# A graph network on one core: the attention's first rows and masks are kept in places of the row work and loaded during the second convolution

## The chip, the cores and the metric

The kernel runs on one core of a Trainium2 chip. The metric is the device time of one execution in microseconds (us), as the median of several runs. The engines are named as in the profile: PE is TensorE (PEld its weight loads), DVE is VectorE, ACT is ScalarE, POOL is GpSimd, and SP is SyncE, which here only issues DMAs. A "q" behind a name (SPq) is the engine's instruction queue.

## The reference

There are N = 6250 nodes with D = 128 features and E = 100000 edges, sorted by their end `dst`. Two graph convolutions run one after the other, then an attention layer; both parts add their input and normalise each row.

```python
def gcn_conv(x, src, dst, ew, W, b):          # with a self loop of weight 1 per node
    deg = segment_sum(ew, dst, N)
    dinv = where(deg > 0, rsqrt(deg), 0)
    h = x @ W
    return segment_sum(h[src] * (dinv[src] * ew * dinv[dst])[:, None], dst, N) + b

h  = sigmoid(gcn_conv(relu(gcn_conv(x, ..., W1, b1)), ..., W2, b2))
x1 = layernorm(x + h)
z, rh = x1 @ fc_w.T, edge_attr @ fc_r_w.T     # attention; aw is attn_w in three rows
e = leaky_relu(z[src] @ aw[0] + z[dst] @ aw[1] + rh @ aw[2], 0.01)
alpha = softmax of e over the edges with the same dst
out = relu(segment_sum(alpha[:, None] * (z[src] + rh), dst, N) + x1 @ loop_w)
return layernorm(x1 + out)
```

## The kernel before

The edges are cut into NC = 49 chunks of CC = 2048, the nodes into NB = 49 blocks of 128 (P). For each chunk, `pick` gathers the source rows in two ways: most of them from a table in SBUF (`hot`, three bfloat16 parts per value) by matmuls with a 0/1 matrix (`mask`, L532, product `g`), the rest by indirect DMA issued by POOL (`far`, L541). `pick` also builds `wm` (L547, L554), the 0/1 matrix of the edges' ends. `scatter` (L578) multiplies the gathered rows with it into a window of 144 nodes, and `add_in` (L583) adds this window to the accumulator. `weigh` (L571) puts the edge weights in. Chunk c is picked while chunk c-1 is scattered. This is done three times: in the first convolution, in the second and in the attention ("conv3").

Whenever a window has moved past some nodes, a `Pieces` object deals out the work that these nodes need next, as generators. `x1_of` is that of the second convolution, for up to four blocks of nodes at a time: multiply by `dinv` (L329), sigmoid (L440), transpose (L444), add (L446), normalise (L411 to L418), transpose (L454), the products with the attention's weights (L463), copies (L466, L467), the product with the loop weights (L471), and the three parts of the next `hot` table (ACT L476, DVE `low` L479 to L481, store `hz` L482). The last two pieces can only be done when the last chunk has been added in.

The second convolution also carries two kinds of work for the attention: `edge_dots` (L1030, L1031), which multiplies each edge's attributes with a vector, and `row_work`, a generator with one step for each of the first chunks. It loads `dst` and `src` by rows, and writes `drow` and `srow` to DRAM (node number within its block, for the ends and the sources), and `rels`, `place` and `blks` to SBUF. Its large tiles are `h_i`, `d_i`, `s_i`, `s_j` (in turn in one place, tag "i", 8 KB in each partition), `h_f`, `d_f` (tag "f", 8 KB) and `s_b` (4 KB), all from the pool `rows2`, which is closed with the second convolution.

The attention's scores are a generator too, `scores`, which runs ahead of the chunks. `ends(c0, n)` loads `dk`, four chunks of `drow` broadcast to all partitions (L1110), compares it with the partition number (L1112), multiplies with the table `a_d` (L1117) and stores `adg` to `adgd`. `starts(c)` does for each half chunk: `sources` loads `rk`, 1024 values of `srow` broadcast (L1105, two half chunks ahead), a comparison (L1138), `ohb` (L1140), 24 matmuls `k` with `adp` (L1145), a product and a sum (`sel`, L1148). `softmax(b)` takes a batch of chunks (2, 5, then 7) from there to `al3` and `aw`, the attention of its edges in two layouts. `shares` (L1254 to L1264) and `edge_part` (L1275 to L1304) use them chunk by chunk, and `pick`, `scatter` and `add_in` work as before with `mask` loaded from `masks` (L1325).

The pools give each tile its number of buffers: three `rk`, one `dk`, two `al3`, two `mask`, two `ohb`.

At the start, the tiles `spread` and `spread_f` (about 1 KB together in each partition) hold a permutation of the partitions, from which `first` (L169) is made. Then the pool `prep` loads `dst_i` (SP), `ew_f` (ACT), `src_i` (SP) and the weights (ACT, L610), and casts `dst_f` (L616, L617), from which `ends` (L622) and all the sorting follow.

What sets the order: outside the second convolution's loop a scheduler orders the instructions of each engine, from its own estimates; only the start of the scores has raised priority. The loop of the second convolution is in `manual_schedule`, in the order in which it is written. Every engine executes its instructions in order, and a wait holds up all that stand behind it.

Of the kernel before, what the change touches and what calls it, by code (L numbers as in the profile page):

```python
# [9 lines left out]
F32 = mybir.dt.float32  # L10
# [9 lines left out]
P = 128  # L20
# [5 lines left out]
TC = 16  # L26
# [12 lines left out]
def gnn_kernel(ctx, tc, x, src, dst, ea, ew, W1, b1, W2, b2, fcw, fcrw, attn, loopw, out):  # L39
# [119 lines left out]
    nc.gpsimd.tensor_copy(behind[:, : P - 1], ident[:, 1:])  # L159


    spread = const.tile([P, P + 1], I32, name="spread")
    for of, at in ((iota_i[:, :P], slice(0, P)), (iotap_i[:, 0:1], slice(P, P + 1))):
        nc.vector.tensor_scalar(spread[:, at], of, 79, None, op0=OP.mult)
        nc.vector.tensor_scalar(spread[:, at], spread[:, at], P - 1, None, op0=OP.bitwise_and)
    spread_f = const.tile([P, P + 1], F32, name="spread_f")
    nc.vector.tensor_copy(spread_f, spread)
    first = const.tile([P, P], BF16, name="first")
    nc.vector.tensor_scalar(first, spread_f[:, :P], spread_f[:, P:], None, op0=OP.is_gt)  # L169

    lower = const.tile([P, TC, TC], BF16, name="lower")
    nc.vector.tensor_tensor(lower, iotab[:, None, :TC].to_broadcast([P, TC, TC]),
# [768 lines left out]


    acc2 = acc1
    with tc.tile_pool(name="conv2", bufs=2) as wp, tc.tile_pool(name="arp", bufs=2) as ap_, \
            tc.tile_pool(name="rows2", bufs=1) as rp, tc.tile_pool(name="x1p", bufs=2) as xp, \
            tc.tile_pool(name="ps_g2", bufs=4, space=PSUM) as ps_g, \
# [1 line left out]


        def row_work():  # L950
            h_i = rp.tile([P, NT, P + 2], I32, name="h_i", tag="i")
            nc.gpsimd.memset(h_i, -1)
            for b, (c0, n) in enumerate(batches):

                at = lambda r: (c0 * NL + r - 1) * P - 1
                rows = [r for r in range(n * NL + 2) if at(r) >= 0 and at(r) + P + 2 <= E]
                r0, m = rows[0], len(rows)
                nc.sync.dma_start(h_i[r0 : r0 + m, b, :], bass.AP(tensor=dst.tensor, offset=dst.offset + at(r0), ap=[[P, m], [1, P + 2]]))
                if b == 0:
                    nc.sync.dma_start(h_i[1:2, b, 1:], dst[None, 0 : P + 1])  # L960
                if b == NT - 1:
                    for r in range(r0 + m, n * NL + 2):
                        if at(r) < E:
                            nc.sync.dma_start(h_i[r : r + 1, b, : E - at(r)], dst[None, at(r) : E])
            yield
            h_f = rp.tile([P, NT, P + 2], F32, name="h_f", tag="f")
            nc.vector.tensor_copy(h_f, h_i)

            nc.vector.scalar_tensor_tensor(same, h_f[:, :, 1:], -0.5, h_f[:, :, : P + 1], op0=OP.max, op1=OP.is_equal)
            yield  # L970
            nc.vector.tensor_scalar(last, same[:, :, 1:], -1.0, 1.0, op0=OP.mult, op1=OP.add)

            filled = rp.tile([P, NT], F32, name="filled")
            nc.vector.tensor_reduce(filled, same[:, :, 1:P], AX.X, OP.min)
            nc.vector.tensor_reduce(odd[:, 3:4], filled, AX.X, OP.max)
            yield
            d_i = rp.tile([NC, CC], I32, name="d_i", tag="i")
            load_rows(nc.sync, d_i, dst)
            yield
            d_f = rp.tile([NC, CC], F32, name="d_f", tag="f")  # L980
# [12 lines left out]
            yield  # L993
            nc.vector.tensor_tensor(dp, dp, off[:, :, None].to_broadcast([NC, NL // 2, 2 * P]), op=OP.subtract)
            offc = rp.tile([NC, NL // 2], F32, name="offc")
            nc.vector.tensor_tensor(offc, off, off[:, 0:1].to_broadcast([NC, NL // 2]), op=OP.subtract)
            yield
            nc.vector.tensor_reduce(odd[:NC, 2:3], d_f, AX.X, OP.max)
            nc.vector.tensor_scalar(odd[:NC, 2:3], odd[:NC, 2:3], float(WS), None, op0=OP.is_ge)
            yield  # L1000
            by_partition(ps_mm, lambda t, ps: nc.scalar.copy(rels[:, :, t], ps), lambda t: ds_[:, t, :])
            ps = ps_mm.tile([P, NL // 8, 64], F32, name="mm")
            for s in range(NL // 2):
                q = s % 4
# [4 lines left out]
            s_i = rp.tile([NC, CC], I32, name="s_i", tag="i")  # L1009
            load_rows(nc.sync, s_i, src)  # L1010
            yield
            nc.vector.tensor_scalar(s_i, s_i, 127, None, op0=OP.bitwise_and)
            s_b = rp.tile([NC, CC], BF16, name="s_b")
            nc.vector.tensor_copy(s_b, s_i)
            nc.sync.dma_start(srow[:, :], s_b)
            yield
            s_j = rp.tile([NC, CC], I32, name="s_j", tag="i")
# [62 lines left out]
    with tc.tile_pool(name="look", bufs=2) as lp, tc.tile_pool(name="conv3", bufs=2) as wp, \  # L1080
# [2 lines left out]
            tc.tile_pool(name="ps_r3", bufs=1, space=PSUM) as ps_r, tc.tile_pool(name="ps_k3", bufs=1, space=PSUM) as ps_k, \  # L1083
            tc.tile_pool(name="ps_c3", bufs=2, space=PSUM) as ps_c:
        MB = max(n for _, n in batches)
        zero = lp.tile([1, P], F32, name="zero", bufs=1)
        nc.vector.memset(zero, 0.0)
        nc.sync.dma_start(adgd[None, 0:P], zero)
        nc.sync.dma_start(adgd[None, (NC * NL + 1) * P :], zero)

        a_d = lp.tile([P, 3, J, NB], BF16, name="a_d", bufs=1)
        for j in range(J):
            ps = ps_c.tile([P, 3, NB], F32, name="rec")
            nc.tensor.matmul(ps, wide[:, P + j : 2 * P + j], adp[:, 1, :, :NB], start=True, stop=j == 0)
# [6 lines left out]
        def sources(i):  # L1101

            if i < 2 * NC:
                rks[i] = lp.tile([P, HC], BF16, name="rk", bufs=3)
                nc.sync.dma_start(rks[i], srow[i // 2, None, i % 2 * HC : (i % 2 + 1) * HC].to_broadcast([P, HC]))  # L1105

        def ends(c0, n):

            dk = lp.tile([P, 4 * P], BF16, name="dk", bufs=1)
            nc.sync.dma_start(dk[:, : n * P], drow[c0 : c0 + n, :].rearrange("(o c) p -> o (c p)", o=1).to_broadcast([P, n * P]))  # L1110
            yield
            nc.vector.tensor_scalar(dk[:, : n * P], dk[:, : n * P], iotap, None, op0=OP.is_equal)  # L1112
# [19 lines left out]
        def starts(c):  # L1132

            for h in range(2):
                of = slice(h * NL // 2, (h + 1) * NL // 2)
                sources(2 * c + h + 2)
                mk = rks.pop(2 * c + h)
                nc.vector.tensor_scalar(mk, mk, iotap, None, op0=OP.is_equal)  # L1138
                ohb = lp.tile([P, NB, NL // 2], BF16, name="ohb")
                nc.vector.tensor_tensor(ohb, iota_t[:, :NB, : NL // 2], blks[:, c, None, of].to_broadcast([P, NB, NL // 2]),  # L1140
                                        op=OP.is_equal)
                ps = ps_k.tile([P, NL // 2, NB], F32, name="k")
                for s in range(NL // 2):
                    for k in range(3):
                        nc.tensor.matmul(ps[:, s, :], mk[:, s * P : (s + 1) * P], adp[:, 0, k, :NB], start=k == 0, stop=k == 2)  # L1145
                yield
                sel = lp.tile([P, NL // 2, NB], F32, name="sel", bufs=1)
                nc.vector.tensor_mul(sel, ps, ohb.rearrange("p b s -> p s b"))  # L1148
                nc.vector.tensor_reduce(asr[:, 1 + c * NL + of.start : 1 + c * NL + of.stop], sel, AX.X, OP.add)
# [3 lines left out]
        def softmax(b):  # L1153
# [65 lines left out]
            yield  # L1219
            aw = lp.tile([P, MB * NL], F32, name="aw")  # L1220
            nc.scalar.copy(aw[:, : n * NL], ps[:, 1 : R - 1])
            al3 = lp.tile([P, MB, TC, 3], BF16, name="al3")
            parts(lambda k: al3[:, :n, :, k], al[:, :n, :], nc.vector)
            ready[b] = al3, aw.rearrange("p (c s) -> p c s", s=NL)

# [83 lines left out]
        for b, (c0, n) in enumerate(batches):  # L1309
# [6 lines left out]
            for c in range(c0, c0 + n):  # L1316
# [4 lines left out]
                    deal(to - done)  # L1321
                    done = to

                mask = wp.tile([P, GP * P], BF16, name="mask", bufs=2)
                nc.sync.dma_start(mask, masks[c])  # L1325
                shares(c, al3, c - c0)
                beside()
# [15 lines left out]
        pieces.go(N, 999)  # L1343
    right_r.close()
    rightA.close()
    hotp.close()


# [174 lines left out]
```

## Time and profile before

| | |
|---|---|
| runs, us | 2397.48, 2405.32, 2406.43, 2407.49, 2418.14 (median 2406.43) |
| profiled execution | 2418.03 us, of which the span is 2416.1 us |
| mean granted TensorE clock | 0.836 |
| busy in the span | PE 1837.7 us, DVE 1659.5, POOL 1043.9, ACT 957.2 |
| DMA | 316.38 MB, mean 131 GB/s |
| stages of the span | start and sorting to 176 us, first convolution to 866, between to 912, second convolution to 1447, between to 1482, scores of the first batch to 1550, attention to 2410 |

How to read it: busy times are sums over one execution, by engine. A stage's own row tells more than the whole: between the stages no engine is busy, and the time is that of a chain in which one waits for the other. The chain of waits follows the work back from the last instruction; a line "DMA a<-b" in it is a transfer that somebody waited for. In the timeline, "[2.75 <-X]" is the idle time of that engine before the instruction and what ended it.

### The profile page before, as it was taken

The page shows a single profiled execution, that of the slowest core. Times are in us where ns is not written, and L with a number is a line of the kernel's source. Part 1 is how long each engine was busy: PE and PEld are TensorE (multiplying, and loading weights), DVE is VectorE, ACT ScalarE, POOL GpSimd, SP SyncE. Part 2 cuts the span into 40 slices and gives each one's busy share as a digit, 9 for nine tenths or more (in the row PEclk, how much of TensorE's full clock was granted, in tenths as well). Part 3 has the DMA queues.
Part 4 walks back from the last instruction along what each step waited for, and adds up shares of the span by engine and source line. Part 5 has one row for each costly group of instructions (what it writes and reads, how often), then busy time and mean ns, then how long its engine had stood idle before and what let it go on. Part 6 is the DMA issues. An engine that isn't in the chain of part 4 may idle for free.

```text
span 2416.1 us, 79261 instructions
## 1 busy us (share of the span) xinstructions
PE 1837.7 (76%) x34061; PEld 1604.9 (66%) x34061; DVE 1659.5 (69%) x3281; ACT 957.2 (40%) x3099; POOL 1043.9 (43%) x941
## 2 busy tenths in 40 slices
PE   3767888878888758788878884587877778888884
PEld 2556777767777647677667673577766767767774
DVE  7895776766767337777777775887876777776552
ACT  1253444443443425465556552033323232424332
POOL 4054345544444526576666652123332233324441
PEclk9778788878888868898888895678888888889887
DMA  2132314232231456666566575446444455544441
GB/s 54 29 109 80 107 52 137 56 119 90 79 121 51 135 182 197 181 187 205 181 191 204 178 204 158 123 115 157 134 145 129 141 139 150 143 133 130 129 131 47
DMA packets 257393, 316.38 MB, mean 131 GB/s; under 512 B 38349, under 2 KB 194131, under 8 KB 249466
## 3 DMA queue, kind: packets, MB, share of 16 engines
q1 hardware_dynamic: 224823, 249.62, 32.8%
q0 software_dynamic: 23520, 48.22, 9.4%
q10 hardware_dynamic: 8688, 13.37, 1.7%
q8 instruction: 270, 4.42, 0.8%
q14 instruction: 92, 0.75, 0.1%
HBM read 265.14 MB, written 45.97 MB: 129 GB/s over the span
## 4 chain that ended last, share of the span: by engine, by line
PE 62%; DVE 14%; issue 13%; ACT 4%; another core or an unknown queue 4%; DMA 2%; POOL 0%; DVEq 0%; ACTq 0%; SPq 0%; POOLq 0%
PE win L578 24%; PE g L532 19%; PE r L758 3%; PE rec L1263 2%; PE r L1293 2%; DVE sel L1148 2%; PE rec L821 2%; PE k L1145 2%; PE rec L1304 2%; ACT got L537 2%; DVE wm L547 1%; DVE put L814 1%; PE mm L383 1%; DVE ohm L809 1%
## 5 line engine op out<-in xcount | busy, mean ns | idle before, releaser
L541 POOL DMA_INDIRECT far<-g,sidx x490 | 694.0, 1416 | 574.5 <-PE win L578 415.0
L532 PE MATMUL g<-hot,mask 128*32 128x128 bf16 x21168 | 578.9, 250 | 279.0 <-issue 257.8
L537 ACT ACTIVATE got<-g,swt 128x128 f32<-128x128 f32 x1764 | 493.5, 377 | 654.8 <-PE g L532 223.2
L532 PEld LDWEIGHTS <-mask 128*32 128x32 bf16 x21168 | 426.8, 111 | 398.2 <-issue 381.0
L541 POOL DMA_INDIRECT far<-zd,sidx x245 | 295.2, 1205 | 631.6 <-PE win L578 526.6
L578 PE MATMUL win<-wm,got 128*128 128x144 f32 x3528 | 556.1, 317 | 10.1 <-DVE acc L583 6.3
L578 PEld LDWEIGHTS win<-wm,got 128*128 128x128 f32 x3528 | 517.6, 215 | 35.3 <-issue 20.5
L547 DVE TENSOR_TENSOR wm<-iota,sdst 128x1728 f32<-128x1728 f32 x147 | 286.6, 1950 | 1.1 <-POOL hot L343 0.8
L571 ACT ACTIVATE wm<-wm,swt 128x64 f32<-128x64 f32 (+1 forms) x735 | 200.8, 353 | 75.3 <-DVE wm L554 38.8
L583 DVE TENSOR_TENSOR acc<-acc,win 128x144 f32 x147 | 44.6, 303 | 218.9 <-PE win L578 211.3
L578 PE MATMUL win<-wm,far 128*128 128x64 f32 (+1 forms) x1470 | 184.4, 272 | 0.0
L578 PEld LDWEIGHTS win<-wm,far 128*128 128x128 f32 x1470 | 180.6, 194 | 0.2 <-ACT got L537 0.2
L1145 PE MATMUL k<-adp,rk 128*128 128x49 bf16 x2352 | 105.6, 200 | 63.9 <-DVE sel L1148 34.7
L1145 PEld LDWEIGHTS <-rk 128*128 128x128 bf16 x2352 | 93.0, 107 | 81.7 <-issue 54.4
L1030 DVE TENSOR_TENSOR et<-et,ar_row 128x2048 f32<-128x2048 f32 (+1 forms) x49 | 111.6, 2278 | 5.4 <-DMA et<-in_edge_attr_dram 5.4
L1031 DVE TENSOR_REDUCE dots<-et 128x16 f32<-128x2048 f32 (+1 forms) x49 | 112.0, 2286 | 1.7
L1148 DVE TENSOR_TENSOR sel<-k,ohb 128x392 f32<-128x392 f32 x98 | 83.8, 855 | 23.2 <-PE k L1145 12.1
L758 PE MATMUL r<-oh,first 128*128 128x48 bf16 x784 | 79.7, 268 | 9.0 <-DVE oh L754 8.0
L809 DVE TENSOR_TENSOR ohm<-iota_t,pm 128x2048 bf16<-128x2048 bf16 x49 | 59.7, 1219 | 38.2 <-PE rec L821 33.3
L1298 ACT COPY sw<-r 128x256 f32<-128x256 f32 (+1 forms) x49 | 18.3, 374 | 161.2 <-PE r L1293 81.5
L758 PEld LDWEIGHTS <-first 128*128 128x128 bf16 x784 | 69.5, 120 | 15.9 <-issue 6.3
L814 DVE TENSOR_TENSOR put<-ohg,rec 128x1360 bf16<-128x1360 bf16 x49 | 77.8, 1588 | 0.0
(408 smaller groups left out, 2295.8 us busy)
## 6 DMA issues: line engine op xcount, KB each, us to landing
et<-in_edge_attr_dram SPq DMA_DIRECT2D x97, 512.0 KB
et<-in_edge_attr_dram SPq DMA_DIRECT2D x48, 1024.0 KB
mask<-masks SPq DMA_DIRECT2D x98, 384.0 KB
rk<-srow SPq DMA_DIRECT2D x98, 256.0 KB
mask<-srd SPq DMA_DIRECT2D x49, 384.0 KB
masks<-mask SPq DMA_DIRECT2D x49, 384.0 KB
far<-g,sidx POOLq DMA_INDIRECT x490
dr<-dinvd SPq DMA_DIRECT2D x22, 256.0 KB
```

The source lines that it names most:

```text
L532: nc.tensor.matmul(ps[32 * q : 32 * q + 32, g, :], mask[:, (g0 + g) * P + 32 * q : (g0 + g) * P + 32 * q + 32], hot[:, 4 * (g0 + g) + q, k ...
L537: nc.scalar.activation(got[:, g, :], ps[:, g, :], AF.Copy, scale=swt[:, c, g0 + g : g0 + g + 1])
L541: nc.gpsimd.indirect_dma_start(out=got, out_offset=None, in_=table[:, :], in_offset=bass.IndirectOffsetOnAxis(ap=sidx[:, c, g : g + 1], ax ...
L547: nc.vector.tensor_tensor(wm[:, : GP * WC].rearrange("p (g w) -> p g w", w=WC), iota[:, None, 1 : WC + 1].to_broadcast([P, GP, WC]), sdst[ ...
L571: nc.scalar.activation(m, m, AF.Copy, scale=swt[:, c, g : g + 1])
L578: nc.tensor.matmul(ps[:, n0 : n0 + m.shape[-1]], rows[g], m, start=g == 0, stop=g == G - 1)
L758: nc.tensor.matmul(ps, first, oh[:, :, t], start=t == 0, stop=t == TC - 1)
L814: nc.vector.tensor_tensor(put[:, :, : G * F].rearrange("p t (g f) -> p t g f", f=F), ohg[:, :, :, None].to_broadcast([P, TC, G, F]), rec[: ...
L1030: nc.vector.tensor_mul(et[:n], et[:n], ar_row[:n, None, :].to_broadcast([n, TC, D]))
L1031: nc.vector.tensor_reduce(dots[:n, c, :], et[:n], AX.X, OP.add)
L1145: nc.tensor.matmul(ps[:, s, :], mk[:, s * P : (s + 1) * P], adp[:, 0, k, :NB], start=k == 0, stop=k == 2)
L1148: nc.vector.tensor_mul(sel, ps, ohb.rearrange("p b s -> p s b"))
```

## The change

- `spread` and `spread_f` move into a pool of their own that is closed when `first` is made. The pool `prep` takes that place over, so the loads into it wait for `first`.
- The large tiles of `row_work` come from a new pool `rowp`, which stays open to the end of the attention. When the row work is done with them, three held tiles take their places: `held_i` (three `rk` and `a_d`), `held_f` (two masks and three `al3`), `held_s` (two `dk` and two `ohb`). The first three `rk`, two `dk` and two `mask` loads depend on nothing of the attention, and the scheduler puts them, and the comparisons on them, into the second convolution.
- `dk` has two places instead of one, `al3` three instead of two. `rk`, `mask` and `ohb` keep their numbers.
- The two DMAs that write zeros to the ends of `adgd` read a zero row of `before` instead of a tile that was set to zero for it. In the program they stand ahead of the second convolution; the scheduler puts them at the front of SP's queue.

```diff
-    spread = const.tile([P, P + 1], I32, name="spread")
...
-    spread_f = const.tile([P, P + 1], F32, name="spread_f")
-    nc.vector.tensor_copy(spread_f, spread)
     first = const.tile([P, P], BF16, name="first")
-    nc.vector.tensor_scalar(first, spread_f[:, :P], spread_f[:, P:], None, op0=OP.is_gt)
+    with tc.tile_pool(name="spread", bufs=1) as spp:
+        spread = spp.tile([P, P + 1], I32, name="spread")
...
+        spread_f = spp.tile([P, P + 1], F32, name="spread_f")
+        nc.vector.tensor_copy(spread_f, spread)
+        nc.vector.tensor_scalar(first, spread_f[:, :P], spread_f[:, P:], None, op0=OP.is_gt)
...
     acc2 = acc1
+
+    leftC = ctx.enter_context(ExitStack())
+    rowp = leftC.enter_context(tc.tile_pool(name="rowp", bufs=1))
+
+    nc.sync.dma_start(adgd[None, 0:P], before[P - 1 :, :])
+    nc.sync.dma_start(adgd[None, (NC * NL + 1) * P :], before[P - 1 :, :])
...
-            h_i = rp.tile([P, NT, P + 2], I32, name="h_i", tag="i")
+            h_i = rowp.tile([P, NT, P + 2], I32, name="h_i", tag="i")
...
-            s_b = rp.tile([NC, CC], BF16, name="s_b")
+            s_b = rowp.tile([NC, CC], BF16, name="s_b", tag="s")
...
-        zero = lp.tile([1, P], F32, name="zero", bufs=1)
-        nc.vector.memset(zero, 0.0)
-        nc.sync.dma_start(adgd[None, 0:P], zero)
-        nc.sync.dma_start(adgd[None, (NC * NL + 1) * P :], zero)
-
-        a_d = lp.tile([P, 3, J, NB], BF16, name="a_d", bufs=1)
+        held_i = rowp.tile([P, 2 * CC], BF16, name="held_i", tag="i")
+        rk3 = held_i[:, : 3 * CC // 2].rearrange("p (k e) -> p k e", k=3)
+        a_d = held_i[:, 3 * CC // 2 : 3 * CC // 2 + 3 * J * NB].rearrange("p (k j b) -> p k j b", k=3, j=J)
+        held_f = rowp.tile([P, 2 * CC], BF16, name="held_f", tag="f")
+        held_s = rowp.tile([P, CC], BF16, name="held_s", tag="s")
+        mask2 = held_f[:, : 2 * GP * P].rearrange("p (k s) -> p k s", k=2)
+        al3s = held_f[:, 2 * GP * P : 2 * GP * P + 3 * MB * TC * 3].rearrange("p (i c t k) -> p i c t k", i=3, c=MB, k=3)
+        dk2 = held_s[:, : 8 * P].rearrange("p (k s) -> p k s", k=2)
+        ohb2 = held_s[:, 8 * P : 8 * P + NB * NL].rearrange("p (k b s) -> p k b s", k=2, b=NB)
+        dks = [0]
...
-                rks[i] = lp.tile([P, HC], BF16, name="rk", bufs=3)
+                rks[i] = rk3[:, i % 3, :]
...
-            dk = lp.tile([P, 4 * P], BF16, name="dk", bufs=1)
+            dk = dk2[:, dks[0] % 2, :]
+            dks[0] += 1
...
-                ohb = lp.tile([P, NB, NL // 2], BF16, name="ohb")
+                ohb = ohb2[:, h]
...
-            al3 = lp.tile([P, MB, TC, 3], BF16, name="al3")
+            al3 = al3s[:, b % 3]
...
-                mask = wp.tile([P, GP * P], BF16, name="mask", bufs=2)
+                mask = mask2[:, c % 2, :]
...
+    leftC.close()
```

`h_f`, `d_i`, `d_f`, `s_i` and `s_j` change their pool in the same way as `h_i`.

More of the change, by code (lines that the diff above doesn't have):

```diff
@@ L159, in gnn_kernel @@
     nc.gpsimd.tensor_copy(behind[:, : P - 1], ident[:, 1:])
-    spread = const.tile([P, P + 1], I32, name="spread")
-    for of, at in ((iota_i[:, :P], slice(0, P)), (iotap_i[:, 0:1], slice(P, P + 1))):
-        nc.vector.tensor_scalar(spread[:, at], of, 79, None, op0=OP.mult)
-        nc.vector.tensor_scalar(spread[:, at], spread[:, at], P - 1, None, op0=OP.bitwise_and)
-    spread_f = const.tile([P, P + 1], F32, name="spread_f")
-    nc.vector.tensor_copy(spread_f, spread)
-    first = const.tile([P, P], BF16, name="first")
-    nc.vector.tensor_scalar(first, spread_f[:, :P], spread_f[:, P:], None, op0=OP.is_gt)
+    first = const.tile([P, P], BF16, name="first")
+    with tc.tile_pool(name="spread", bufs=1) as spp:
+        spread = spp.tile([P, P + 1], I32, name="spread")
+        for of, at in ((iota_i[:, :P], slice(0, P)), (iotap_i[:, 0:1], slice(P, P + 1))):
+            nc.vector.tensor_scalar(spread[:, at], of, 79, None, op0=OP.mult)
+            nc.vector.tensor_scalar(spread[:, at], spread[:, at], P - 1, None, op0=OP.bitwise_and)
+        spread_f = spp.tile([P, P + 1], F32, name="spread_f")
+        nc.vector.tensor_copy(spread_f, spread)
+        nc.vector.tensor_scalar(first, spread_f[:, :P], spread_f[:, P:], None, op0=OP.is_gt)
     lower = const.tile([P, TC, TC], BF16, name="lower")
@@ L965, in row_work @@
             yield
-            h_f = rp.tile([P, NT, P + 2], F32, name="h_f", tag="f")
+            h_f = rowp.tile([P, NT, P + 2], F32, name="h_f", tag="f")
             nc.vector.tensor_copy(h_f, h_i)
@@ L976, in row_work @@
             yield
-            d_i = rp.tile([NC, CC], I32, name="d_i", tag="i")
+            d_i = rowp.tile([NC, CC], I32, name="d_i", tag="i")
             load_rows(nc.sync, d_i, dst)
             yield
-            d_f = rp.tile([NC, CC], F32, name="d_f", tag="f")
+            d_f = rowp.tile([NC, CC], F32, name="d_f", tag="f")
             nc.vector.tensor_copy(d_f, d_i)
@@ L1008, in row_work @@
             yield
-            s_i = rp.tile([NC, CC], I32, name="s_i", tag="i")
+            s_i = rowp.tile([NC, CC], I32, name="s_i", tag="i")
             load_rows(nc.sync, s_i, src)
@@ L1016, in row_work @@
             yield
-            s_j = rp.tile([NC, CC], I32, name="s_j", tag="i")
+            s_j = rowp.tile([NC, CC], I32, name="s_j", tag="i")
             load_rows(nc.sync, s_j, src)
```

## The prediction

> **What bounds the kernel now.** I read the page's busy times first, then one row per stage, then the chain of waits inside the stages that the change touches, and last the timeline of single engines.
>
> ```profile
> PE 1837.7 (76%) x34061; PEld 1604.9 (66%) x34061; DVE 1659.5 (69%) x3281; ACT 957.2 (40%) x3099; POOL 1043.9 (43%) x941
> ...
> PE 62%; DVE 14%; issue 13%; ACT 4%; another core or an unknown queue 4%; DMA 2%; POOL 0%; DVEq 0%; ACTq 0%; SPq 0%; POOLq 0%
> ```
>
> TensorE carries the kernel as a whole; DMA is 2% of the chain. A change to a few loads can only pay where one of them ends a wait. The stages (columns: window, length, busy time of PE, PEld, DVE, ACT, POOL with counts, granted clock, DMA share, GB/s):
>
> ```profile
> 912.00:1447.00 535.00, 437.89 (x8743) 380.26 (x8734) 399.19 (x440) 299.49 (x959) 353.25 (x233) 0.88 0.61 190
> 1447.00:1482.00 35.00, 13.62 (x138) 8.35 (x137) 17.20 (x52) 13.52 (x25) 0.00 (x0) 0.60 0.38 123
> 1482.00:1550.00 68.00, 37.72 (x744) 31.87 (x745) 52.35 (x143) 8.54 (x28) 16.30 (x12) 0.58 0.58 166
> ```
>
> The second convolution (912 to 1447) keeps TensorE 82% busy, VectorE 75%. Between it and the attention (1447 to 1482) no engine is half busy: that is a chain of latencies. The chain of waits there:
>
> ```profile
> 1443.18 3.98 PE win L578 x34
> 1447.57 6.28 DMA rk<-srow
> 1454.91 1.95 DVE wm L547
> 1456.86 0.60 DVE low L479
> ...
> 1485.80 6.37 DMA rk<-srow
> ...
> 1540.47 5.48 DMA dk<-drow
> ```
>
> So the first `rk` load stands on the chain, and so does a `dk` load 90 us later. VectorE and TensorE at these places (idle time before, and its cause, in brackets):
>
> ```profile
> 1453.23 0.49 DVE L1138 TENSOR_SCALAR rk<-rk,iotap 128x1024 bf16<-128x1024 bf16 x1 [2.75 <-DMA rk<-srow]
> 1456.77 0.68 DVE L479 TENSOR_TENSOR low<-zrows,part 128x512 f32<-128x512 f32 x1
> 1546.29 0.25 PE L1117 MATMUL rec<-a_d,dk 128*128 128x18 bf16 x3 [2.53 <-DVE dk L1112]
> ```
>
> VectorE idles only 2.75 us for the load, but the masks of two `rk` and one `dk` and a `wm` build stand in its queue ahead of `low` (L479), on which the last pieces of the second layer's output depend. The end of that chain, the first `k` matmul at 1480.75, starts the attention.
>
> **Part 1, the start of the kernel.** `spread` no longer has a place of its own; `dst_i` and `ew_f` take it over and so wait for its reader `first` (L169). In the changed program's order SP issues the two `adgd` stores, then `dst_i`; ACT issues two weights and three 512 KB tiles of x ahead of `ew_f`, with three more weights and the table load queued behind its wait, and the two small tails of `dst_i` wait for two of the x tiles to land.
>
> ```profile
> 0.75 0.40 SPq L237 DMA_DIRECT2D dst_i<-in_dst_dram  x1
> 7.25 0.26 DVE L169 TENSOR_SCALAR first<-spread_f 128x128 bf16<-128x128 f32 x1
> 13.14 1.04 ACT L616 CAST dst_f<-dst_i 49x1024 f32<-49x1024 int32 x1
> 14.21 0.87 DVE L622 COPY ends<-dst_f 49x2 f32<-49x2 f32 x1 [6.57 <-ACT dst_f L616]
> ```
>
> `dst_i` goes out at about 7.1 instead of 0.75, and took at most 5.9 us (VectorE casts its half at 6.62): there at 13. The table load (1.28) and the cast (1.04) then follow, instead of running at 11.84 to 14.18: `dst_f` ends at 15.3 at the earliest, +1.1. The three x tiles are 1.57 MB. The window 6 to 10 moved 140 GB/s at a DMA share of 0.65, so some 215 GB/s at full share: 7.3 us from about 3, landed near 10.5. The last tail goes out then; a small load took 4.6 (`vecs`, issued at 1.57, read by TensorE at 6.13), so it is there at 15.1 and `dst_f` ends at 17.4: +3.2. At the bare 140 GB/s the tiles take 11.2 us, and it is +7. I take +4, since `dst_i` shares the engines with them. `src_i`, behind the tails, goes out near 11 instead of 2.25; its cast (18.77) moves behind the edge weights' copies, and TensorE reads it at 22.80, so I count nothing for it, at worst its 1.90 us. The page "DMA: Bandwidth & Descriptors" of the Trainium skill (section "Anatomy of one DMA — SWDGE (gpsimd) path") fits 2.0 us plus bytes at 436 GB/s, for a path that is not this one: by it the tiles land near 8.6, the tails are early and the term is +1.1; the traced rate decides. VectorE is full from 14 to 57 (32.67 of 37 us from 20 on), and its new order brings parts of the later work 1.1 to 1.4 us earlier. Net: +3, from -0.3 to +6. POOL gets its degree memset (5.42) and index copies (2.36) ahead of 147 `lim` memsets, which then end near 17.5; L636 reads them at 18.85 before, some 4 later now: covered by 1.3 to 5 us, and late by as much as the cover falls short.
>
> **Part 2, inside the second convolution.** Added to VectorE: two `dk` masks (0.31, 0.35), three `rk` masks (0.48 each), two `ohb` (0.55 the pair): 2.7 us in five chunks of some 11 us. VectorE waits 1.2 to 2.6 us in each for TensorE there ("2.63 <-PE win L578" at 1074.40), so this is covered; uncovered it costs 2.7. The loads (0.77 MB `rk`, 0.2 `dk`, 0.79 masks) go into a stage with a DMA share of 0.61. SP's queue: the first `dk` load stands until the `srow` store of 1016.11 has landed, with the `s_j` loads behind it, which VectorE reads only at 1037.85; the three `rk` loads stand until `d_f` is cast (1048.27 to 1049.48), with the `hz` store behind, whose data are ready at 1052.8. Their masks come 9 us after their issue, against 6.3 us of landing. Take +0.5, from 0 to +2.7. The page "SBUF — State Buffer" (section "SBUF: two separate sides") says that VectorE in some modes locks GpSimd out of a shared port for a whole instruction, which speaks against masks placed beside GpSimd's gathers. By it up to 2.7 us of gathers slip; GpSimd is idle 182 of 535 us here, so the sum by it stays the same within its range.
>
> **Part 3, the boundary.** From 1447.82 VectorE has left ahead of `low`: `bias`, `wm`, its small part, `wm`: 0.14 + 1.86 + 0.41 + 1.86 = 4.27 us by the starts of these rows. `low` starts at 1452.1 instead of 1456.77: -4.7, and the third `rk` mask behind it gives 0.4 more. What is late next: `low` waits for ACT, which first copies L471's product (ended 1448.09). With its mask already there, TensorE now has 39 of conv3's `g` matmuls (29 ns each, since 105 took 3.04 us at 1457.02: 1.1 us) ahead of L471, among the last scatter, and they wait for the first and second `hot` load; 68 more ahead of L444 wait for the third. Those go out at 1435.15, 1438.71, 1443.43 with 1.18 MB each. At 203 to 356 GB/s, the slices of this stretch, each takes 3.3 to 5.8 us: second landed by 1442 to 1447, third by 1445 to 1453. L444 is due at 1455.3. So I take -4.7, from 0 (the loads hold TensorE) to -5.1. The zero memset and the two stores that go from here are off the chain. The fourth `rk` load (1485.80, 6.37 us) still waits for a place and stays.
>
> **Part 4, the attention.** With two places for `dk` the load of 1540.47 goes out when the batch before last is used, well ahead. TensorE idles 2.53 us for it, VectorE 1.55; the chain shows 5.48. Take -2.3, from 0 to -5.5. VectorE waits for `dk` 5.0 us more in five places; the other late readers there are TensorE's, so I take 30%, -1.5, from 0 to -5. A third `al3` removes no wait that a row shows. The order of the first chunks is reshuffled by the scheduler; no row prices that: 4 us either way.
>
> **Sum.** +3 + 0.5 - 4.7 - 2.3 - 1.5 = -5.0. The profiled execution took 2418.03 (span 2416.1 and 1.9 around it), so such a run becomes 2413; it lies 11.6 above the median of 2406.43, so the median becomes 2401.5.
>
> **Rivals.** *Nothing at the boundary* (0.17): the `x1` pieces are latencies of ACT, TensorE and VectorE, and if `hot` holds TensorE the 4.7 go: 2406. For it: 143 GB/s is the mean from 1425 to 1485, and at that rate the third load lands at 1460. Against: the slices above.
> *All waits recovered* (0.20): start -0.3, boundary -5.1, the two `dk` terms -5.5 and -5: -15.9, 2390.5. For it: the chain carries the whole `dk` load. Against: TensorE idled only half of it.
> *A worse order in conv3* (0.15): the scheduler moves `k` blocks across `g` and scatter blocks on TensorE, which executes in order. From 1550 on TensorE waits 52.0 us at `g`, 40.8 at the edge sums, 23.0 and 19.4 at `k`: 135 us. 15% more is +20, so +15 in all: 2421. From 4% (+5) it decides the sign. For it: half of these waits are of exactly that kind. Against: the instructions are the same, and after the first batches the two orders run alike.
> That slices of one held tile wait for one another (0.03) would also make it slower; in the built order each waits for its own slot.
>
> **How the numbers follow.** My sum has 0.45. All ends at once give -20 and +13; four fifths of that, -16 to +10, is 2390 to 2416, and with a part of the rivals 2389 to 2417. A measurement of this kernel tells about 0.5% (12 us) from no change. Faster by more: 0.20 and 0.07 of my own case's end; slower by more: 0.15 and 0.03; the rest, 0.55, within.
>
> **What would show it.** `ends` (L622) near 18 instead of 14.21; no `rk` wait at the boundary and `low` near 4 to 5 us sooner after the last scatter; the `rk` masks near 1058 to 1068 without a wait; no `dk` wait at 1546. I am wrong if conv3's length (1482 to the end) grows, if conv2 grows by more than 3 us, or if TensorE stands at a `g` matmul ahead of the last scatter.

## The result, and the profile after

The changed kernel takes 2416.65 us (median of 52 runs, 2394.2 to 2437.5) beside 2409.54 for the kernel before on the same chips (94 runs): a ratio of 1.0029, 95% interval 1.0016 to 1.0042. It is about 7 us slower; the forecast was 5 us faster. The time lies in the forecast's range, but on the other side of the kernel before. The profiled execution took 2422.36 us, its span 2420.4, at a granted clock of 0.838 (0.836 before). Every ratio here compares only runs within 1.5% of the fastest of the same kernel; beside `e1_spread_right`, `e2_spread_alone`, `e16_right_again` and `e17_late_ohb_again` this leaves out 9 of 23 runs of the kernel before and none of the 12 runs beside them, and the medians of all runs would give 0.9982, 1.0022, 0.9989 and 0.9981. The page's busy times and chain after:

```profile
PE 1829.0 (76%) x34061; PEld 1597.2 (66%) x34061; DVE 1659.1 (69%) x3280; ACT 955.2 (39%) x3099; POOL 1042.6 (43%) x941
...
PE 62%; DVE 16%; issue 13%; another core or an unknown queue 3%; ACT 3%; DMA 2%; POOL 0%; DVEq 0%; ACTq 0%; SPq 0%; POOLq 0%
```

No engine does more work than before, so whatever was lost lies in waits. The same stages (from the second border on 2 to 3 us later; columns as before):

```profile
912.00:1450.00 538.00, 434.10 (x8775) 374.47 (x8775) 400.78 (x446) 299.98 (x964) 351.98 (x233) 0.88 0.61 192
1450.00:1484.00 34.00, 16.72 (x151) 10.87 (x151) 14.16 (x40) 14.72 (x31) 0.00 (x0) 0.67 0.34 96
1484.00:1552.00 68.00, 39.68 (x764) 34.35 (x764) 53.76 (x150) 8.49 (x29) 16.59 (x13) 0.56 0.59 172
```

These rows hardly differ from those of before. The chain of waits at the boundary does:

```profile
1455.20 0.34 PE win L579 x2
1456.38 1.31 DVE wm L548
...
1458.65 1.87 DVE wm L548
1460.52 0.60 DVE low L480
...
1489.18 7.59 DMA held_i<-srow
```

The transfer `rk<-srow` that stood here for 6.28 us is gone: the last scatter is followed by `wm` and `low` at once. The later one (6.37 us before, 7.59 now) has stayed. Engine by engine (VectorE and TensorE rows of the timeline):

```profile
1455.57 0.30 DVE L584 TENSOR_TENSOR acc<-acc,win 128x144 f32 x1 [4.59 <-PE win L579]
1460.45 0.68 DVE L480 TENSOR_TENSOR low<-zrows,part 128x512 f32<-128x512 f32 x1
1543.09 0.24 PE L1130 MATMUL rec<-held_i,held_s 128*128 128x18 bf16 x3
```

`low` starts 4.88 us after the last `add_in`, where it was 9.59 (1447.18 to 1456.77), and TensorE's matmul on `dk` has lost its wait of 2.53. So both waits that were forecast to go are gone. The start does not do what was forecast:

```profile
5.08 4.94 DVE L169 CAST spread_f<-spread 128x129 f32<-128x129 int32 x1
10.40 0.36 SPq L238 DMA_DIRECT2D dst_i<-in_dst_dram  x1
20.12 0.68 DVE L618 CAST dst_f<-dst_i 49x1024 f32<-49x1024 int32 x1 [9.40 <-DMA dst_i<-in_dst_dram]
23.08 1.04 ACT L617 CAST dst_f<-dst_i 49x1024 f32<-49x1024 int32 x1
24.15 0.16 DVE L623 COPY ends<-dst_f 49x2 f32<-49x2 f32 x1 [3.35 <-ACT dst_f L617]
```

`ends` runs at 24.15 instead of 14.21, and the first `add_in` of the first convolution at 211.70 instead of 200.56. Two things are new. The cast of `spread`, 0.22 us before, takes 4.94. And `dst_i` needs 9.7 us from its issue to its cast, against at most 5.9 before. GpSimd's rows for the first, of the kernel before and then of the changed one:

```profile
9.64 5.42 POOL L860 MEMSET acc<- 3x6394 f32 x1
```

```profile
4.38 5.57 POOL L861 MEMSET acc<- 3x6394 f32 x1
```

The scheduler put this memset, on three partitions, ahead of the 147 small ones. The cast of `spread` ends at 10.02, 0.07 us after the memset.

To follow a loss past the start I number the `add_in` rows (147 of them, and the attention's edge sums, 196 in all) and compare times between these marks. The 61st and 63rd are the twelfth and fourteenth of the second convolution, the 97th is its last but one. The 103rd is the third edge sum; the expectations below call it the fifth, since it is the fifth mark of the attention. Within a stage they move by several microseconds from one execution to the next, even in code that did not change, so only short stretches are used.

| us between marks | start to 1st | 61st to 63rd (early `ohb`) | 97th to 98th (last scatter) | 97th to 103rd (boundary, first batch) | 103rd to last |
|---|---|---|---|---|---|
| before | 200.56 | 21.54 | 3.05 | 151.91 | 790.50 |
| after | 211.70 | 25.44 | 4.90 | 145.15 | 794.79 |
| `e0_before_again` | 202.63 | 22.40 | 3.05 | 152.38 | 794.08 |
| `e2_spread_alone` | 209.96 | 20.54 | 4.32 | 151.41 | 775.41 |
| `e7_two_dk_alone` | 199.81 | 23.84 | 4.40 | 149.08 | 789.42 |
| `e1_spread_right` | 203.05 | 27.19 | 4.88 | 145.80 | 776.28 |
| `e3_memset_pieces` | 211.65 | 25.45 | 4.87 | 145.24 | 769.36 |
| `e6_ew_behind_dst` | 209.49 | 21.38 | 4.89 | 145.66 | 772.64 |
| `e4_one_dk` | 203.17 | 25.43 | 4.88 | 147.57 | 787.69 |
| `e13_late_ohb` | 204.78 | 20.74 | 4.89 | 147.13 | 792.93 |

### The profile page after: what moved, and what is told of

It is laid out like the page before. It is cut to its first block, busy times and chain, and to the rows that moved or that the text cites. A ratio compares the mean times of both kernels' runs of the same rounds, so it can differ in the third digit from the quotient of the medians.

```text
span 2420.4 us, 79271 instructions
## 1 busy us (share of the span) xinstructions
PE 1829.0 (76%) x34061; PEld 1597.2 (66%) x34061; DVE 1659.1 (69%) x3280; ACT 955.2 (39%) x3099; POOL 1042.6 (43%) x941
## 4 chain that ended last, share of the span: by engine, by line
PE 62%; DVE 16%; issue 13%; another core or an unknown queue 3%; ACT 3%; DMA 2%; POOL 0%; DVEq 0%; ACTq 0%; SPq 0%; POOLq 0%
PE win L579 25%; PE g L533 18%; PE r L759 3%; PE k L1158 2%; DVE sel L1161 2%; PE rec L1276 2%; PE r L1306 2%; PE rec L822 2%; DVE wm L548 2%; PE rec L1317 2%; DVE put L815 1%; PE mm L384 1%; ACT got L538 1%; DVE ohm L810 1%
## 5 line engine op out<-in xcount | busy, mean ns | idle before, releaser
L542 POOL DMA_INDIRECT far<-zd,sidx x245 | 297.1, 1213 | 626.5 <-PE win L579 525.6
L533 PE MATMUL g<-hot,mask 128*32 128x128 bf16 x14112 | 379.8, 246 | 223.7 <-issue 195.6
L533 PEld LDWEIGHTS <-mask 128*32 128x32 bf16 x14112 | 277.8, 109 | 312.8 <-issue 302.0
L533 PE MATMUL g<-hot,held_f 128*32 128x128 bf16 x7056 | 194.9, 250 | 62.8 <-issue 60.4
L572 ACT ACTIVATE wm<-wm,swt 128x64 f32<-128x64 f32 (+1 forms) x735 | 201.0, 353 | 73.1 <-DVE swt L1277 32.8
L533 PEld LDWEIGHTS <-held_f 128*32 128x32 bf16 x7056 | 142.2, 110 | 96.8 <-issue 89.8
L1158 PE MATMUL k<-adp,held_i 128*128 128x49 bf16 x2352 | 103.2, 200 | 61.3 <-DVE sel L1161 39.2
L1158 PEld LDWEIGHTS <-held_i 128*128 128x128 bf16 x2352 | 91.9, 107 | 78.1 <-issue 46.3
L1161 DVE TENSOR_TENSOR sel<-k,held_s 128x392 f32<-128x392 f32 x98 | 83.6, 853 | 21.4 <-PE k L1158 10.5
L1317 PE MATMUL rec<-pl,sw 128*128 128x144 f32 x196 | 46.0, 367 | 49.2 <-ACT sw L1311 37.4
```

The source lines that it names most:

```text
L533: nc.tensor.matmul(ps[32 * q : 32 * q + 32, g, :], mask[:, (g0 + g) * P + 32 * q : (g0 + g) * P + 32 * q + 32], hot[:, 4 * (g0 + g) + q, k ...
L542: nc.gpsimd.indirect_dma_start(out=got, out_offset=None, in_=table[:, :], in_offset=bass.IndirectOffsetOnAxis(ap=sidx[:, c, g : g + 1], ax ...
L572: nc.scalar.activation(m, m, AF.Copy, scale=swt[:, c, g : g + 1])
L1317: nc.tensor.matmul(ps, sw[:p, g, :], pl[:p, g, :], start=g == 0, stop=g == len(sizes) - 1)
```

## The experiments

The theory: the start is lost to the place of `spread` and costs more than the boundary and `dk` bring. The rivals: the third convolution runs in a worse order, or the loads and comparisons cost the second convolution its gain.

**The start undone, the rest kept** (`e1_spread_right`). The temporary pool goes to the other side of memory, so that `prep` does not take its place:

```diff
-    with tc.tile_pool(name="spread", bufs=1) as spp:
+    with tc.tile_pool(name="spread", bufs=1, side="right") as spp:
```

> The changed kernel with the temporary pool of spread on the other side of SBUF, so that the loads of dst_i and ew_f take over no place and wait for nothing; all else as changed. Theory A (the start is the loss, the attention gains): dst_i goes out at 0.75 and ends is copied near 14 instead of 24.15; the first add of the first convolution comes near 200.6 as before the change instead of 211.7; the boundary and the first batch keep their gain of some 6 to 7 us; the second convolution keeps a loss of 2 to 6. Time 2 to 8 us under the kernel before (ratio 0.997 to 0.999). Rival B (the gain at the boundary is an accident of the clock, the start was given back in the first convolution): ratio 1.000 or more.

Measured: ratio 0.9988 (0.9952 to 1.0024). `dst_i` goes out at 0.75 again, `ends` starts at 14.28, the first `add_in` is at 203.05, and the boundary keeps its 145.80. The rows settle the start; the time does not decide between the two theories, since its interval holds 1.

**The start alone** (`e2_spread_alone`). The kernel before, with only the temporary pool of the change:

```diff
-    spread = const.tile([P, P + 1], I32, name="spread")
+    with tc.tile_pool(name="spread", bufs=1) as spp:
+        spread = spp.tile([P, P + 1], I32, name="spread")
```

> The kernel before with only the temporary pool of spread, so that the loads wait for first; nothing of the attention is changed. Theory A: ends near 24 instead of 14.21, the first add near 211 instead of 200.6, time 9 to 11 us over the kernel before (ratio 1.004 to 1.0046). Rival B (later stages give the start back, or the two stores at the head of SP's queue make the delay): ends near 18 or the ratio under 1.002.

Measured on the same chip: 1.0047 (1.0012 to 1.0083), 11 us by the ratio, with the same rows as in the changed kernel:

```profile
5.08 4.94 DVE L169 CAST spread_f<-spread 128x129 f32<-128x129 int32 x1
24.32 0.16 DVE L623 COPY ends<-dst_f 49x2 f32<-49x2 f32 x1 [2.51 <-ACT dst_f L617]
```

By this ratio, this part of the change makes the kernel slower by itself, and without it the changed kernel is not slower by anything that the measurement can tell. The two ratios multiply to 1.0035; the whole change measured 1.0029.

**The memset in pieces** (`e3_memset_pieces`), to see whether it is what holds the cast:

```diff
-        nc.gpsimd.memset(deg3, 0.0)
+        for m0 in range(0, NP, 800):
+            nc.gpsimd.memset(deg3[:, m0 : min(m0 + 800, NP)], 0.0)
```

> The changed kernel with POOL's memset of the degree accumulator (3 x 6394) cut into eight of 800 columns. Theory A (VectorE's cast of spread_f is held by one GpSimd instruction for as long as that one lasts): the cast takes at most 1 us instead of 4.94, dst_i goes out near 6 instead of 10.40, and ends comes 3 to 4 us sooner than 24.15. Rival C (the cast is slow as long as GpSimd writes at all): the cast still takes 4 to 5 us. Rival D (the cast waits for its input and GpSimd has no part): 4.9 us.

```profile
5.08 0.28 DVE L169 CAST spread_f<-spread 128x129 f32<-128x129 int32 x1
16.60 0.69 DVE L618 CAST dst_f<-dst_i 49x1024 f32<-49x1024 int32 x1 [10.55 <-DMA dst_i<-in_dst_dram]
23.03 0.16 DVE L623 COPY ends<-dst_f 49x2 f32<-49x2 f32 x1 [5.74 <-ACT dst_f L617]
4.37 0.90 POOL L862 MEMSET acc<- 3x800 f32 x1
```

The cast takes 0.28 us beside a short memset: it is the long one that held it. The time is not recovered, though. `dst_i` goes out at 5.74, 4.66 us earlier, and then lies beside the x tiles and `ew_f` for 10.9 us until VectorE's cast; its last tail goes out only at 14.54, and ScalarE, whose cast needs it, starts at 20.66. So `ends` comes only 1.1 us sooner, and the first `add_in` not at all. The expectation was a miss: I had taken the landing time as fixed.

**The transfer beside it moved away** (`e6_ew_behind_dst`). The changed kernel, with `ew_f` on SP's queue behind `dst_i`:

```diff
-        load_rows(nc.scalar, ew_f, ew)
+        load_rows(nc.sync, ew_f, ew)
```

> The changed kernel with the edge weights' load issued by SP behind dst_i instead of by ACT at the same time. Theory A (dst_i takes 9.7 us because ew_f and src_i share the DMA engines with it from 10.4 on): dst_i lands 5 to 7 us after its issue, VectorE's cast of its half comes near 16.5 instead of 20.12. Rival E (such a load takes 9 to 10 us whatever runs beside it): 20 as before.

```profile
10.40 0.37 SPq L238 DMA_DIRECT2D dst_i<-in_dst_dram  x1
16.08 0.69 DVE L618 CAST dst_f<-dst_i 49x1024 f32<-49x1024 int32 x1 [5.37 <-DMA dst_i<-in_dst_dram]
20.10 0.16 DVE L623 COPY ends<-dst_f 49x2 f32<-49x2 f32 x1 [3.33 <-ACT dst_f L617]
```

Issued at the same 10.40, `dst_i` lands in 5.7 us instead of 9.7. Here `ew_f` goes out at 11.80, 1.4 us behind `dst_i` instead of beside it, and `src_i` at 16.91 instead of 11.81. So 4.0 us of the start are the loads sent together, which the wait for `first` had lined up; which of the two counts more, this run does not tell. `ends` gains 4.05, the first `add_in` 2.2 of it, about as much as that mark differs between two profiles of the kernel before. The other 5.9 of the 9.9 by which `ends` is late stay with the late issue.

**The `dk` places** (`e7_two_dk_alone`: the kernel before with two; `e4_one_dk`: `e1_spread_right` with one), beside a second profile of the kernel before (`e0_before_again`).

```diff
-            dk = lp.tile([P, 4 * P], BF16, name="dk", bufs=1)
+            dk = lp.tile([P, 4 * P], BF16, name="dk", bufs=2)
...
-            dk = dk2[:, dks[0] % 2, :]
+            dk = dk2[:, 0, :]
```

> The kernel before with two places for dk and nothing else. Theory A: the stretch from the last add but one to the fifth edge sum is 149 to 150 us instead of 151.9, and TensorE's wait of 2.53 us for dk is gone; the wait for the first rk load at the boundary stays. Rival G: 151 to 152.

> The changed kernel with spread on the other side of SBUF and one place for dk instead of two. Theory A (2.3 us or more of the gain come from the second place): TensorE waits 2 to 3 us again for a dk load near the third ends, and the stretch from the last add but one to the fifth edge sum is 147.5 to 149.5 us instead of 145.8. Rival G (all the gain is the boundary's): 145 to 146.5.

> The kernel before once more, for the lengths of its stages on this chip. Theory A: the stretch from the last add but one to the fifth edge sum is 151 to 153 us as in the first profile, the first add comes at 200 to 203; the stages in between differ by several us with the granted clock alone.

From the 97th to the 103rd mark `e7_two_dk_alone` takes 149.08 us, 2.8 less than the 151.9 of the three kernels with one `dk` and the old loads. `e4_one_dk` takes 147.57, 1.8 more than `e1_spread_right`. Both agree on some 2 us. Only one of the two shows the wait that should be behind it: in `e7_two_dk_alone` TensorE's 2.53 us for `dk` are gone, but in `e4_one_dk` TensorE waits 0.33 us for it at most, so there no row accounts for the 1.8. `e0_before_again` shows how far marks can be trusted: the stretch of the boundary agrees within 0.5 us, the start within 2.1, the attention within 3.6.

**The first `ohb` later** (`e13_late_ohb`). In the changed kernel VectorE's first `ohb` stands in the second convolution ahead of the last part of a `hot` table and an `add_in`:

```profile
1054.90 0.36 DVE L1153 TENSOR_TENSOR held_s<-iota_t,blks 128x392 bf16<-128x392 bf16 x1 [1.61 <-issue]
1055.18 0.69 DVE L482 TENSOR_TENSOR part<-low,part 128x512 bf16<-128x512 f32 x1
1055.79 0.30 DVE L584 TENSOR_TENSOR acc<-acc,win 128x144 f32 x1
```

It waits 1.61 us, here without a named releaser; in `e1_spread_right` the same row reads "[2.27 <-ACT blks L1030]", the copies of `blks` that ScalarE makes. The experiment adds to `e1_spread_right` a comparison that also reads zeros made from the last `dots`, so that it cannot stand so early, and the memset in pieces (not shown here):

```diff
+        late = lp.tile([P, 1], F32, name="late", bufs=1)
+        nc.vector.tensor_scalar(late, dots[:, NC - 1, 0:1], 0.0, None, op0=OP.mult)
...
+                if c == 0:
+                    nc.vector.scalar_tensor_tensor(ohb, iota_t[:, :NB, : NL // 2], late, blks[:, c, None, of].to_broadcast([P, NB, NL // 2]),
+                                                   op0=OP.add, op1=OP.is_equal)
```

> The changed kernel with spread on the other side of SBUF, with the first two ohb made to depend on a value of the last chunk's dots, so that VectorE builds them at the boundary and not in the second convolution, and with POOL's memset of the degree accumulator in eight pieces. Theory A (in the changed kernel VectorE stood 1.61 us for ACT's copies of blks in front of the first ohb, with an add of the second convolution queued behind): no such wait near the thirteenth chunk; from the twelfth to the fourteenth add 21.5 to 22.5 us (before the change 21.5, changed 25.4); the boundary and the first batch, from the last add but one to the fifth edge sum, stay at 145 to 147 us (before 151.9, changed 145.2); ends takes under 0.9 us. Time 4 to 10 us under the kernel before (0.996 to 0.998). Rival F (the slow chunks there are the clock): 24 to 26 us again, time as with spread on the other side alone, 0.9988.

Measured: 0.9974 (0.9941 to 1.0006). The wait is gone, and the 61st to 63rd mark take 20.74 us; the boundary takes 147.13, some 1.7 more than with the early `ohb`. `ends` takes 0.65 us (1.80 in `e1_spread_right`), though the first `add_in` comes no sooner. Of the five builds of this table with the early `ohb`, four take 25.4 to 27.2 there (mean of the five 25.0); the four kernels with the old loads take 20.5 to 23.8 (mean 22.1). That is 3 us on the mean, but it doesn't follow the wait: `e3_memset_pieces` waits 0.32 us and takes 25.45, `e6_ew_behind_dst` waits 1.22 and takes 21.38. By the 67th mark the means lie 0.9 us apart. So the early comparison costs from 0 to 3 us, and the marks settle it no closer.

**Repeats and a middle place.** `e15_changed_again` is the changed kernel; `e14_mid_ohb` is `e13_late_ohb` with `late` taken from `dots[:, 20, 0:1]`, so that the comparison stands in the middle of the second convolution. `e16_right_again` and `e17_late_ohb_again` repeat `e1_spread_right` and `e13_late_ohb`. These four ran where the granted clock was higher (0.89 to 0.90) and the kernel before takes 2003 us.

> The changed kernel once more beside it, on the same chip. Theory A: first add at 209 to 212, twelfth to fourteenth add near 25, the stretch at the boundary 145 to 146; 4 to 10 us over the kernel before (1.002 to 1.004). Rival H: within 0.1% of the kernel before.

> As the last version, but the first two ohb depend on a value of chunk 20's dots, so that VectorE builds them within the second convolution, five chunks later than in the changed kernel, when blks has long been written. Theory A: no wait in front of them; from the twelfth to the fourteenth add 20.5 to 23.8 us; the stretch from the last add but one to the fifth edge sum back at 145 to 146 (147.1 with the late ohb); first add at 200 to 205. By these stretches 6 us under the kernel before (ratio 0.9965 to 0.9985) and 12 to 15 under the changed kernel. Rival H (the stretches do not add up in the whole time, other stages give it back): ratio 0.999 or more.

> The changed kernel with the temporary pool of the dealing's segment lists on the other side, a second time, to tell what the change is worth once the start is as before. Theory A (the start alone made the changed kernel slower, the rest of the change is worth what the marks between the last sum of the second convolution and the fifth of the third showed, -6, against +3 at the early place comparison): 0.9988, within 0.9975 to 1.000. Rival B (the forecast's own terms without the start, -8.0 of 2406): 0.9967. Rival C (the time saved at the boundary is given back in the third convolution, so that nothing is left): 1.0000 and more.

> The same with the first place comparison held until the edges' row work of the second convolution is through, and the memory set in pieces, beside the run above on the same chip. Theory A (the early comparison's wait for its input costs about 3): 3 us below the run above, 0.9975. Rival D (its wait was covered by the scatter's matmuls on TensorE): the same as the run above. In the profile both should give 145 to 147.5 us from the last sum but one of the second convolution to the fifth of the third.

| | ratio to before | 95% interval |
|---|---|---|
| `e15_changed_again` | 1.0033 | 1.0005 to 1.0061 |
| `e14_mid_ohb` | 1.0010 | 0.9976 to 1.0044 |
| `e16_right_again` | 1.0019 | 0.9982 to 1.0056 |
| `e17_late_ohb_again` | 0.9973 | 0.9942 to 1.0004 |

The changed kernel is slower there too, by the same share. The marks, which were expected as at the lower clock, are shorter: in `e15_changed_again` the first `add_in` comes at 207.87, the 61st to 63rd mark take 21.26 us and the boundary 139.53. The repaired start, the late `ohb` and the memset in pieces together come out 0.27% below the kernel before at both clocks; the mean of 0.9974 and 0.9973 has a half-width of sqrt(0.0033² + 0.0031²)/2 = 0.0023, which is faster than before by 0.04 to 0.50%, an interval that only just leaves out no change. The repaired start alone gives 0.9988 and 1.0019, mean 1.0003 ± 0.0026: no difference from the kernel before that shows, and its interval still overlaps with that of the changed kernel's 1.0029. For `e16_right_again` 0.9975 to 1.000 was expected. There the start is repaired by the marks (first `add_in` at 194.17, 13.7 us ahead of `e15_changed_again`), but the ratio lies only 0.0014, 3 us, below that of the changed kernel. The middle place missed its expectation, and in its profile the last scatter waits for a gather as well ("2.76 <-DMA far<-g,sidx"; the 97th to 98th mark take 7.91 us there, 8.47 in `e17_late_ohb_again`, 4.89 in `e15_changed_again`). At this clock `e16_right_again`'s first `ohb` shows no wait, and `e14_mid_ohb`'s first `add_in`, 14.8 us ahead of `e15_changed_again`'s, is 2.1 us behind it by the 61st mark. From 450 to 700 us the granted clock was 0.90 in the former and 0.95 in the latter. With one profiled execution of each, that is no proof that the clock took the gain back; the timed ratios are what counts.

## Why the prediction was wrong

**Part 1 is the step that failed.** It counted +3 for the start (at most +6); the first `add_in` is 9.7 us later in the four builds with the late loads than in the kernels before (mean 210.7 against 201.0), and `e2_spread_alone` measured +11 in the whole time for it alone. (The three builds of the table with `spread` on the other side come to 203.7, so by them 7.0 of the 9.7 go with the place of `spread`; what is left is no more than the 2.8 by which the kernels before differ among themselves.) Three pieces of that step were wrong. *The issue*: `dst_i` was taken to go out at 7.1, near the 7.25 at which `first` ran before. It went out at 10.40 (without the long memset, in `e3_memset_pieces`, at 5.74), because the memset that I had listed as a load on GpSimd ("ahead of 147 `lim` memsets") was in front of GpSimd's queue at 4.38 and held up VectorE's cast. *The landing*: I used 5.9 us from a trace in which `dst_i` went out at 0.75 and `ew_f` at 1.88, 1.1 us behind it; with both sent at the same instant `dst_i` took 9.7. *The bound*: I had it in the small tails behind the x tiles (17.4). With the late issue they went out directly, at 10.81 and 11.13; only in `e3_memset_pieces`, where `dst_i` is early, does the last of them wait (14.54).

The row that shows the hold-up stood in the trace of before already: `ends`, a copy of 98 numbers, took 0.87 us there and ended at 15.08, 0.02 us after the memset (9.64 + 5.42 = 15.06). In the changed kernel, where the memset is over, it takes 0.16; in `e1_spread_right` it takes 1.80 and again ends 0.02 after the memset:

```profile
14.28 1.80 DVE L623 COPY ends<-dst_f 49x2 f32<-49x2 f32 x1 [6.34 <-ACT dst_f L617]
14.36 2.28 DVE L708 TENSOR_TENSOR dst_i<-dst_f 49x2047 int32<-49x2047 f32 x1
10.64 5.42 POOL L861 MEMSET acc<- 3x6394 f32 x1
```

The Trainium skill's page "SBUF — State Buffer", section "SBUF: two separate sides", says that of a VectorE instruction in a mode that uses the shared port and a GpSimd instruction, whichever starts first has the port for its whole length and the other one is blocked. The rows above agree, to 0.02 and 0.07 us. Not every VectorE instruction is held, though: the TENSOR_TENSOR behind the copy takes 2.28 us beside the memset, and 2.28 in the changed kernel, where no memset runs beside it. The prediction weighed this rule in one direction only (VectorE blocking GpSimd's gathers) and in the second convolution, where nothing came of it (GpSimd's gathers there take 1511 ns on the mean, 1516 before); it belonged at the start, in the other direction.

**Part 2** took +0.5 (to +2.7) with the comparisons covered by VectorE's waits. The three `rk` comparisons did run without a wait (1061.07, 1070.47, 1071.73), and the loads cost nothing that shows. But the first `ohb` needs `blks` from ScalarE, which I had not looked up, and waits 0.3 to 2.3 us for it in the builds of the first table (not at all in `e15_changed_again` and `e16_right_again`). What that costs is from 0 to 3 us by the marks; the runs with the late `ohb` (0.9973 ± 0.0023 against 1.0003 ± 0.0026) point to a cost, but the intervals overlap, and these builds have the memset in pieces as well, which no run takes apart from the late `ohb`. Whether the second convolution grew by more than 3 us can't be read from single profiles: from its first to its last but one `add_in` it takes 530.5 us in the changed kernel, 525.6 and 521.1 in two profiles of the kernel before, and 508.8 in `e1_spread_right`.

**Part 3** is right in its mechanism, and too high in its size. `low` comes 4.71 us sooner after the last `add_in` and the first `k` 4.91 (28.66 us after it instead of 33.57), for -4.7. But that counts from the last `add_in`, which itself comes later: from the 97th mark to the first `k` it is 33.56 us instead of 36.62, a gain of 3.1. What I had as hidden was the 39 `g` matmuls ahead of the last scatter's end. In fact 25 stand among it, and the scatter takes 1.85 us longer (4.90 against 3.05 in both profiles of the kernel before; `e2_spread_alone` and `e7_two_dk_alone`, without them, take 4.32 and 4.40, but there a gather is awaited for 1.13 and 1.21):

```profile
1452.60 0.40 PE L533 MATMUL g<-hot,held_f 128*32 128x128 bf16 x14
1452.93 0.46 PE L579 MATMUL win<-wm,far 128*128 128x96 f32 x2
...
1458.62 0.69 PE L533 MATMUL g<-hot,held_f 128*32 128x128 bf16 x36 [1.58 <-DMA hot<-hz]
```

The last row is the wait for the third `hot` load that the prediction feared. It ends before TensorE is needed at 1463.76, so the rival "nothing at the boundary" falls.

**Part 4** took -2.3 and -1.5. Two places for `dk` measured -2.8 and -1.8 us in the two experiments; a `dk` load of 5.88 us is still on the chain at 1542.94. VectorE's later waits for `dk`, 5.0 us before, are gone from its rows, but no run shows what the -1.5 for them is worth. Of the two parts, -7.0 fall into the stretch from the 97th to the 103rd mark (the -1.5 lies later); it shrank by 6.4, from 151.9 to 145.5 (the mean of `after`, `e1_spread_right`, `e3_memset_pieces` and `e6_ew_behind_dst`), the scatter's 1.85 included.

**The sum** of what the marks show: +9.7 at the start, 0 to +3 at the early `ohb`, -6.4 at the boundary and in the first batch: +3 to +6, against the ratio's 0.0029 × 2409.54 = 7 (3.9 to 10.1). The rival "a worse order in conv3" has nothing for it: from the 103rd mark on the changed kernel takes 794.79 us, the kernel before 790.50 and 794.08. The four groups of TensorE's waits that made up its 135 us come to 131.4, where it needed 155; with the one group that grew (at the edge sums without a named releaser, 1.6 before and 11.5 now) they are 142.9 against 136.8, and 132.1 in `e1_spread_right`, which has the same order. A few us either way remain possible, since this stretch moves by 25 us between the builds of the table. What stays open is whether the rest of the change gains anything by itself: the marks leave 3 to 6 us (6.4 less 0 to 3), while the two timed ratios of the repaired start, 1.0003 ± 0.0026, are +0.7 us with 6 to either side, which holds that gain and its absence.

## What to carry to other kernels

A tile that gives up its own place hands its address to the next one, and loads that had no predecessor then wait for the tile's last reader: price the load's new company and the reader's neighbours on the other engines, not only the reader. When a scheduler moves a long GpSimd instruction, look for the VectorE copies that now run beside it, and in the trace of before for a copy that takes longer than its size: that is the same hold-up in small. A comparison that is moved earlier needs each of its inputs traced to its writer, since a load that has landed is only one of them.

## What the runs showed of the hardware that was not expected

A GpSimd memset on 3 partitions holds a VectorE cast on 128 until it ends: 4.94 us against 0.22, and 0.28 beside pieces of 0.90. A load of 49 partitions (`dst_i`) takes 5.7 us from its issue to its first reader when the next one of its size goes out 1.4 us behind it, and 9.5 to 10.9 when that goes out at the same instant (10.9 with the x tiles beside them).
